# Keys' features in blocks of 432 keys, and two layer norms applied on GpSimd from SBUF

## The chip, the cores and the metric

The kernel runs on one core of a Trainium2 chip. The time is the device time of one execution in microseconds. A "slot", a "unit" and a "batch" below are stretches of this kernel's own main loop.

## What is computed

The input is x of shape (8, 128, 36, 36) in float32: 8 batches, 128 channels, N = 1296 positions. Two layers follow one another; only what the change touches is kept here.

```python
# layer 0: group norm, then convolutions with softmax attention; its sum with x
x = x + conv_attention(group_norm(x))
t = tokens(x)                                # (8, 1296, 128)
# layer 1, first half: additive attention over all pairs of tokens
h = layer_norm(t)                            # mean and variance over the 128 channels
q, k = h @ Wq.T + bq, h @ Wk.T + bk
scores = einsum('bijd,d->bij', tanh(q[:, :, None] + k[:, None]), w) + bw
t = t + softmax(scores) @ h
# layer 1, second half: each of 64 experts takes its best 8 tokens of the batch
h = layer_norm(t)
probs = softmax(h @ gate_w.T, axis=1); topv, topi = top_8(probs)
pooled = sum of topv * h[topi]               # per expert
out = t + scatter(expert_mlp(pooled) * topv)
```

The kernel doesn't evaluate the tanh of every pair. It writes the score as a sum of quotients of products of "features", exponentials of linear maps of the query's and of the key's token. There are NF = 8 groups of 128 features each for queries (`qf`) and for keys (`kf`).

## The kernel before

The main loop goes over 8 batches, 3 chunks of 432 queries (`CH`), and 11 tiles of keys (`KT`): ten of 128 keys and one of 16 (`REM`), which stands sixth in the order. One pass over (batch, chunk, tile) is a unit. A unit of a full tile has 12 slots, that of the small one has two. A batch has 366 slots.

In a slot, TensorE makes two denominators `d` (L910, for three slots ahead, `LAG`) and two numerators `n` (L910); ScalarE takes the logarithm of `d` (L933) and, every second slot, the exponential that inverts (L936); VectorE multiplies `n` by it. In slots 0, 1, 3, 4, 6, 7, 9 and 10 VectorE makes two products into `rp` (L964), and GpSimd adds them to `accp` (L971, L973). In slots 2, 5, 8 and 11 (`DVE_PAIRS`) VectorE also adds, into `accd` (L958, L960), and GpSimd gets no addition. `rp` has three buffers. At a unit's end GpSimd folds the sums (L980, L982), and seven slots later ScalarE makes the weights `e` (L993).

All other work is background, written as Python generators in four lanes: `first_of_all`, `urgent` (attention outputs; for batch 0 also its keys), `gates` (the gating of the batch before), and `background` (layer 0, tokens and keys of the next batch). Each generator yields whether its next step has matmuls and how many slots to rest. `take_turns` (called at the head of a slot) runs steps without matmuls, though not in `DVE_PAIRS` slots except for the first lane. `matmul_turn` (at the end of a slot) runs at most one step with matmuls, paced by a balance of `PACE` = 400 columns a slot. Engines follow the order in which instructions are so recorded, and each engine's queue runs in that order. Matmul results of the background (`aux`) and the numerators `n` share four PSUM banks.

The pieces that the change touches:

- `tokens(b)` turns x into tokens in groups of four transposes (`tpl`, L285), copies them to `tok` in SBUF (L605), takes mean and variance, and has GpSimd raise the variance to the power -1/2 (`ln_rs`, L262). Then it transposes x a second time, two tiles a group (`tpn`), and VectorE normalises from PSUM into `xh` (L640). `xh` is turned back (`tpc`) into `xT`.
- `keys(b, tiles)` makes the keys' features tile by tile: two groups of four matmuls of 128 columns (`pk`, L281), one exponential of 128x512 for each (L684), one write to DRAM (`kd`, L695). For the small tile GpSimd writes two masked copies (L689). The loop's `prefetch` reads a tile back as `kf` (L893), 4 KB a row, two units ahead.
- `gate_logits(b, chunks)` turns the tokens after attention (`t2`) to `t2T` (L790), writes that to DRAM, turns it back two tiles a group (`tp`, L285), and VectorE normalises from PSUM (L800), which needs GpSimd's power `t_rs` (L262). Then it is turned again for the gate's logits.
- `query_block` makes the next chunk's query features in the last units of a chunk: ScalarE L707, GpSimd L708. L372 scales a weight on GpSimd. L468 is layer 0's exponential, `px` one of its matmuls of 432 columns.
- `inner(g)` adds the experts' first bias by a matmul with 16 rows of `ident`.

Before the loop the kernel makes batch 0's tokens, the keys of the first three tiles and three query blocks; the other eight tiles' keys go into `urgent`.

Of the kernel before, what the change touches and what calls it, by code (L numbers as in the profile page):

```python
# [16 lines left out]
N = H * W  # L17
# [53 lines left out]
def kernel(  # L71
# [41 lines left out]
        return t  # L113


    kd = [dram.tile([NKT, 128, NF * 128], F32, tag=f"kd{b % 2}", name=f"kd{b}") for b in range(NB)]
# [10 lines left out]
    with ExitStack() as loop, ExitStack() as score:  # L127
# [139 lines left out]


        TAKE = (False, 1)

        def step(rest=1):
            return (False, rest)
# [311 lines left out]
        prepared, made = {}, set()  # L584

        def tokens(b):

# [39 lines left out]
            rsqrt(rs, ve)  # L627
            xh = big_tile("xh")[:, : NKT * (C + 1)].rearrange("p (t c) -> p t c", c=C + 1)
            nc.gpsimd.memset(xh[:, :, C : C + 1], 1.0)
            yield matmuls(3)  # L630
            for g in range(0, NKT, 2):
                tp = aux("tpn")
                some = list(range(g, min(g + 2, NKT)))
                for t in some:
                    o, n = KT[t]
                    turned_to(tp[:n, (t - g) * C : (t - g + 1) * C], r[:, o : o + n], ident)
                yield TAKE
                for t in some:
# [25 lines left out]
        def keys(b, tiles):  # L664

            xT = prepared[b][1]
            yield matmuls(1)
            for t in tiles:
                o, n = KT[t]
                first = (b, t) == (0, order[0])  # L670
                if first:
                    kf_of[0] = kfp.tile([128, NF, 128], F32, tag="kf", name="kf")
                for q0 in (0, NF // 2):
                    some = slice(q0, q0 + NF // 2)
                    pk = aux("pk1").rearrange("p (q t) -> p q t", t=128)
                    for q in range(NF // 2):
                        bmm(pk[:, q, :n], a_k[:, (q0 + q) * 128 : (q0 + q + 1) * 128],
                           xT[:, o : o + n], start=True, stop=True)
                    yield TAKE
                    if first:  # L680
                        ks = kf_of[0][:, some, :]
                    else:
                        ks = kstp.tile([128, NF // 2, 128], F32, tag="ks", name="ks")
                    nc.scalar.activation(ks[:, :, :n], pk[:, :, :n], AF.Exp)  # L684
                    kd3 = kd[b][t].rearrange("p (q t) -> p q t", t=128)[:, some, :]
                    if n == REM:

                        for x in range(2):
                            nc.gpsimd.tensor_scalar(  # L689
                                ks[:, :, (x + 1) * n : (x + 2) * n], ks[:, :, :n],  # L690
                                pairs[:, min(q0, 1), x : x + 1], None, ALU.mult,
                            )
                        nc.sync.dma_start(kd3[:, :, : 2 * n], ks[:, :, n : 3 * n])
                    else:
                        nc.sync.dma_start(kd3, ks)  # L695
                    if q0 > 0:
                        made.add((b, t))
                    yield matmuls()

        def query_block(b, c, q, qf):  # L700

# [61 lines left out]
        def gate_logits(b, chunks):  # L763


            t2, mv = attended[b]
            if b not in logits:
                logits[b] = (
                    big_tile("probs")[:E, :N],
                    small.tile([E, NCH], F32, tag="mx", name="mx"),  # L770
                )
            pr, mx = logits[b]
            tiles = range(chunks[0] * TPC, (chunks[-1] + 1) * TPC)
            yield step()
# [12 lines left out]
            for c in chunks:  # L787
                tp, tt = turned(c, "t2T")
                yield TAKE
                nc.vector.tensor_copy(tt, tp[:, :CH])  # L790
                nc.sync.dma_start(t2d[b][:, c * CH : (c + 1) * CH], tt)
                yield matmuls(1)
                for j0 in range(0, TPC, 2):
                    tp = aux("tp3")
                    for j in (j0, j0 + 1):
                        turned_to(tp[:T, j * C : (j + 1) * C], tt[:, j * T : (j + 1) * T], ident)
                    yield TAKE
                    for j in (j0, j0 + 1):
                        t = c * TPC + j
                        nc.vector.tensor_scalar(  # L800
                            t2[:T, t, :], tp[:T, j * C : (j + 1) * C],
                            mv[:, t, 0:1], rs[:, t - tiles[0] : t - tiles[0] + 1],
                            ALU.subtract, ALU.mult,
                        )
                    yield matmuls()
            for c in chunks:
                tp, xc = turned(c, "xc")
                yield TAKE
                nc.vector.tensor_copy(xc, tp[:, :CH])
                yield matmuls(2)  # L810
                pg = aux("pg")
                bmm(pg[:E, :CH], gw_s, xc, start=True, stop=True)
                yield TAKE
                nc.vector.tensor_scalar(
                    pr[:, c * CH : (c + 1) * CH], pg[:E, :CH], gb_s, None, ALU.add, ALU.max,
                    accum_out=mx[:, c : c + 1],
                )
                yield matmuls()
# [68 lines left out]
        def prefetch(u):  # L887
            if u < len(units) and u not in kf_of:
                b, c, j = units[u]
                assert (b, j) in made  # L890
                n = 128 if j < NKT - 1 else 32
                kf = kfp.tile([128, NF, 128], F32, tag="kf", name="kf")
                nc.sync.dma_start(  # L893
                    kf[:, :, :n], kd[b][j].rearrange("p (q t) -> p q t", t=128)[:, :, :n]
                )
                kf_of[u] = kf

# [231 lines left out]

        urgent.run(len(slots))  # L1130
        experts = [load_experts(g) for g in range(4)]
        b1_s = biases.tile([NGR, EG, HID], F32, tag="b1", name="b1_s")
        nc.sync.dma_start(b1_s, weight1[:, 128, :].rearrange("(g q) h -> g q h", q=EG))
# [28 lines left out]
    def inner(g):  # L1162
        ph = aux("phid")
        for q in range(EG):
            mm(ph[32 * q : 32 * q + 32, :], pooled_s[:, g * EG + q, :], experts[g][0][:, q, :],
               start=True, stop=False)
        of_group = ident[:NGR, g : g + 1].to_broadcast([NGR, 32])
        for q in range(EG):
            mm(ph[32 * q : 32 * q + 32, :], of_group, b1_s[:, q, :], start=False, stop=True)
# [122 lines left out]
```

## Time and profile before

| | |
|---|---|
| median of 3 runs | 6157.78 us (6153.82 to 6159.6) |
| the profiled execution's own time | 6152.63 us |
| its span, first to last instruction | 6150.6 us |
| granted TensorE clock, mean | 0.986 |
| first numerator of the loop starts at | 158.8 us |
| batch 6, from its first numerator to batch 7's | 736.4 us |
| batch 7, the same to its last numerators | 653.9 us |

In the profile PE is TensorE's matmuls, PEld its weight loads, DVE VectorE, ACT ScalarE, POOL GpSimd and SP the engine that issues the DMAs. A row of a timeline has start, length, engine, line, operation and tiles; the bracket is the idle time before it and who ended that. A row of groups has count, busy time, mean time of one in ns, and idle time before. Rows of stretches have the length, then busy time and count by engine, then granted clock, share of DMA and GB/s.

### The profile page before, as it was taken

How to read it: one execution, taken by the hardware profiler on the slowest of the kernel's cores; microseconds unless marked ns; L12 is line 12 of the kernel's file. 1: busy time of each engine (PE TensorE's matmuls, PEld its weight loads, DVE VectorE, ACT ScalarE, POOL GpSimd, SP SyncE). 2: the span in 40 equal slices, each digit the busy share in tenths (PEclk: the TensorE clock that was granted, in tenths of full speed). 3: DMA queues.
4: the chain of work that ended last, by engine and by line, in shares of the span. 5: the costliest groups of instructions: out<-in, count | busy, mean ns of one | idle time of the engine just before them, and what ended most of it. 6: DMA issues, size and time to landing. Idle time of an engine off the chain costs nothing.

```text
span 6150.6 us, 93223 instructions
## 1 busy us (share of the span) xinstructions
PE 5963.4 (97%) x33576; PEld 2866.4 (47%) x33576; DVE 4798.4 (78%) x9518; ACT 5281.1 (86%) x5371; POOL 4597.5 (75%) x2804
## 2 busy tenths in 40 slices
PE   7999999999999999999999999999999999999996
PEld 5454444544544445444445444454454444544443
DVE  4787878878787787877888777887778878788872
ACT  1888898888988899888998899888898888999980
POOL 4777777777778777878687777877777777787870
PEclk9999999999999999999999999999999999999997
DMA  1200011000210001100111001100021000100017
GB/s 47 71 33 22 25 62 52 20 25 28 72 38 24 26 32 64 42 22 23 49 52 37 22 20 63 45 33 22 28 71 39 24 26 27 61 29 29 25 71 262
DMA packets 150239, 270.88 MB, mean 44 GB/s; under 512 B 45392, under 2 KB 74960, under 8 KB 149776
## 3 DMA queue, kind: packets, MB, share of 16 engines
q1 hardware_dynamic: 149776, 264.92, 12.9%
q8 instruction: 265, 4.34, 0.3%
q14 instruction: 198, 1.62, 0.1%
HBM read 200.41 MB, written 64.19 MB: 43 GB/s over the span
## 4 chain that ended last, share of the span: by engine, by line
PE 76%; ACT 8%; DVE 6%; issue 6%; POOL 2%; DMA 1%; SPq 1%; POOLq 0%; DVEq 0%; ACTq 0%
PE n L910 37%; PE d L910 12%; PE pa L281 7%; ACT lq L933 6%; PE pc L281 5%; PE s L281 3%; PE pk L281 3%; PE pq L281 3%; DVE rp L964 2%; DVE n L958 1%; DVE accd L960 1%; PE d L915 1%; ACT lq L936 1%; PE n L915 1%; ACT e L993 1%
## 5 line engine op out<-in xcount | busy, mean ns | idle before, releaser
L973 POOL TENSOR_TENSOR accp<-accp,rp 128x864 f32<-128x864 f32 x1440 | 2917.0, 2026 | 1032.0 <-DVE rp L964 938.9
L910 PE MATMUL n<-qf,kf 32*128 32x432 f32 (+1 forms) x11520 | 3320.8, 573 | 47.6 <-ACT e L993 13.3
L910 PE MATMUL d<-qf,kf 32*128 32x432 f32 (+1 forms) x11520 | 2983.8, 560 | 39.5 <-ACT lq L933 38.9
L933 ACT ACTIVATE lq<-d 128x864 f32<-128x864 f32 x2928 | 2525.3, 879 | 531.2 <-PE d L910 502.6
L964 DVE TENSOR_TENSOR rp<-n,lq 128x432 f32<-128x432 f32 x3912 | 2174.4, 600 | 739.8 <-PE d L910 539.9
L936 ACT ACTIVATE lq<-lq 128x1728 f32<-128x1728 f32 (+1 forms) x1464 | 2398.2, 1638 | 46.3
L910 PEld LDWEIGHTS n<-qf,kf 32*128 32x128 f32 (+1 forms) x11520 | 1207.1, 184 | 1603.2 <-DVE rp L964 584.0
L910 PEld LDWEIGHTS d<-qf,kf 32*128 32x128 f32 (+1 forms) x11520 | 1088.6, 185 | 420.9 <-issue 225.0
L958 DVE TENSOR_TENSOR n<-n,lq 128x432 f32<-128x432 f32 x1440 | 815.2, 608 | 138.7 <-PE n L910 83.7
L960 DVE TENSOR_TENSOR accd<-n,accd 128x432 f32<-128x432 f32 x1440 | 867.4, 602 | 24.7
L971 POOL TENSOR_TENSOR accp<-rp 128x864 f32<-128x864 f32 x240 | 485.5, 2023 | 194.7 <-DVE rp L964 192.0
L708 POOL TENSOR_SCALAR qf<-qf,cs_s 128x432 f32<-128x432 f32 x192 | 261.2, 1366 | 45.1 <-ACT qf L707 44.4
L281 PEld LDWEIGHTS pa<-xh,e 128*108 128x108 f32 x1920 | 226.1, 176 | 123.7 <-DVE rp L964 53.3
L982 POOL TENSOR_TENSOR accd<-accp,accd 128x432 f32<-128x432 f32 x240 | 265.3, 1106 | 18.8
L980 POOL TENSOR_TENSOR accp<-accp 128x432 f32<-128x432 f32 x240 | 264.6, 1103 | 16.7
L281 PE MATMUL pa<-xh,e 128*108 128x129 f32 x1920 | 265.4, 286 | 6.0 <-DVE accd L960 3.1
L281 PE MATMUL s<-q,k 128*116 128x432 f32 x480 | 230.3, 568 | 1.7 <-DVE q L313 1.4
L281 PEld LDWEIGHTS pk<-xT,a_k 128*128 128x128 f32 x1408 | 171.4, 192 | 107.0 <-DVE n L958 33.7
L459 POOL TENSOR_TENSOR tot<-tot,e 116x432 f32<-116x432 f32 x192 | 212.2, 1105 | 6.0 <-ACT e L468 4.6
L468 ACT ACTIVATE e<-s 116x432 f32<-116x432 f32 x240 | 125.0, 521 | 96.7 <-PE s L281 96.3
L281 PE MATMUL pa<-e,vw 116*128 116x432 f32 x480 | 204.6, 549 | 0.0
L281 PE MATMUL pk<-xT,a_k 128*128 128x128 f32 (+1 forms) x1408 | 202.6, 287 | 0.1
(212 smaller groups left out, 3786.5 us busy)
## 6 DMA issues: line engine op xcount, KB each, us to landing
kf<-kd SPq DMA_DIRECT2D x239, 512.0 KB
kd<-ks SPq DMA_DIRECT2D x158, 256.0 KB
w<-in_weight_dram SPq DMA_DIRECT2D x32, 1024.0 KB
wk_t<-wk_t_d SPq DMA_DIRECT2D x7, 768.0 KB
wv_t<-wv_t_d SPq DMA_DIRECT2D x7, 768.0 KB
wq_t<-wq_t_d SPq DMA_DIRECT2D x7, 768.0 KB
x<-in_x_dram SPq DMA_DIRECT2D x8, 648.0 KB
t<-tokd SPq DMA_DIRECT2D x96, 54.0 KB
```

The costliest lines, as they stand in the source:

```text
L281: mm(out, lhsT, rhs, **kw)
L708: nc.gpsimd.tensor_scalar(qf[:, 1, :], qf[:, 0, :], cs_s[:, q : q + 1], None, ALU.mult)
L910: mm(outs[h][:, :CH], kf[rows[h], q, :], qf_of[b, c, q][rows[h], part, :], start=True, stop=True)
L933: nc.scalar.activation(lq[:, o : o + n, :], d[:, :n, :CH], AF.Ln)
L936: nc.scalar.activation(some, some, AF.Exp, scale=-1.0)
L958: mult(ns[h], ns[h], lq[:, o + h, :])
L960: nc.vector.tensor_add(live["d"], ns[h], live["d"])
L964: mult(rp[:, h, :], n, lq[:, o + h, :])
L971: nc.gpsimd.tensor_add(live["p"], live["r"], rp)
L973: nc.gpsimd.tensor_add(live["p"], live["p"], rp)
L980: nc.gpsimd.tensor_add(s[:, 0, :], s[:, 0, :], s[:, 1, :])
L982: nc.gpsimd.tensor_add(d, s[:, 0, :], d)
```

## The change

`keys` now takes a range of keys instead of tiles: for each of the 8 groups of features one matmul of up to 432 columns, one exponential and one write. `kd` is laid out by features and keys, so that a tile is read back in rows of 512 B. The small tile's two masked copies go to a tile of their own (`kr`), written once to `krd`, in 16 GpSimd operations of 16 columns instead of 4 of 64. Batch 0's first four tiles are made before the loop, by one call for 128 keys and one for 384; the rest are three generators in `urgent`.

`tokens` normalises `tok` from SBUF by GpSimd, and `gate_logits` normalises `t2` in place by GpSimd (the very last chunk by VectorE). The second transposes are gone. These steps yield a new mark, `ASIDE`, and run after the `take_turns` of `DVE_PAIRS` slots alone. The experts' first bias is kept as 64 rows and added by a matmul with 64 rows.

```diff
+        ASIDE = (None, 1)
...
             xh = big_tile("xh")[:, : NKT * (C + 1)].rearrange("p (t c) -> p t c", c=C + 1)
             nc.gpsimd.memset(xh[:, :, C : C + 1], 1.0)
-            yield matmuls(3)
-            for g in range(0, NKT, 2):
-                tp = aux("tpn")
-                some = list(range(g, min(g + 2, NKT)))
-                for t in some:
-                    o, n = KT[t]
-                    turned_to(tp[:n, (t - g) * C : (t - g + 1) * C], r[:, o : o + n], ident)
-                yield TAKE
-                for t in some:
-                    n = KT[t][1]
-                    nc.vector.tensor_scalar(
-                        xh[:n, t, :C], tp[:n, (t - g) * C : (t - g + 1) * C],
-                        mv[:n, t, 0:1], rs[:n, t : t + 1], ALU.subtract, ALU.mult,
-                    )
-                yield matmuls()
+            yield ASIDE
+            for t, (o, n) in enumerate(KT):
+                nc.gpsimd.tensor_scalar(
+                    xh[:n, t, :C], tok[:n, t, :], mv[:n, t, 0:1], rs[:n, t : t + 1],
+                    ALU.subtract, ALU.mult,
+                )
+                if t % 3 == 2 or t == NKT - 1:
+                    yield ASIDE if t < NKT - 1 else step()
...
+        def keys(b, lo, hi):
...
+            for q in range(NF):
+                pk = aux("pk1")[:, :n]
+                bmm(pk, a_k[:, q * 128 : (q + 1) * 128], xT[:, lo:hi], start=True, stop=True)
+                yield TAKE
+                ks = kf_of[0][:, q, :] if first else kstp.tile(
+                    [128, CH], F32, tag="ks", name="ks")[:, :n]
+                nc.scalar.activation(ks, pk, AF.Exp)
+                nc.sync.dma_start(kd[b][:, q, lo:hi], ks)
+                if hi == N:
+                    for x in range(2):
+                        nc.gpsimd.tensor_scalar(
+                            kr[:, q, x, :], ks[:, n - REM :],
+                            pairs[:, q // (NF // 2), x : x + 1], None, ALU.mult,
+                        )
+                yield matmuls()
+            if hi == N:
+                nc.sync.dma_start(krd[b], kr.rearrange("p q x t -> p q (x t)"))
...
                 nc.sync.dma_start(t2d[b][:, c * CH : (c + 1) * CH], tt)
-                yield matmuls(1)
-                for j0 in range(0, TPC, 2):
-                    tp = aux("tp3")
-                    for j in (j0, j0 + 1):
-                        turned_to(tp[:T, j * C : (j + 1) * C], tt[:, j * T : (j + 1) * T], ident)
-                    yield TAKE
-                    for j in (j0, j0 + 1):
-                        t = c * TPC + j
-                        nc.vector.tensor_scalar(
-                            t2[:T, t, :], tp[:T, j * C : (j + 1) * C],
-                            mv[:, t, 0:1], rs[:, t - tiles[0] : t - tiles[0] + 1],
-                            ALU.subtract, ALU.mult,
-                        )
-                    yield matmuls()
+                yield matmuls()
+            yield ASIDE
+            eng = nc.vector if chunks[0] == NCH - 1 else nc.gpsimd
+            for c in chunks:
+                for t in range(c * TPC, (c + 1) * TPC):
+                    eng.tensor_scalar(
+                        t2[:T, t, :], t2[:T, t, :], mv[:, t, 0:1],
+                        rs[:, t - tiles[0] : t - tiles[0] + 1], ALU.subtract, ALU.mult,
+                    )
+                yield ASIDE if c < chunks[-1] else step()
+            yield matmuls(1)
...
             for lane in lanes:
-                if lane.due(p, False) and (k not in DVE_PAIRS or lane is first_of_all):
+                if k not in DVE_PAIRS or lane is first_of_all:
+                    if lane.due(p, False):
+                        lane.run(p)
+                elif lane.due(p, None):
                     lane.run(p)
...
-        drain(tokens(0), keys(0, order[:1]))
+        drain(tokens(0), keys(0, 0, 128))
...
-        drain(keys(0, order[1:3]))
+        drain(keys(0, 128, 512))
         prefetch(1)
-        urgent.append(keys(0, order[3:]))
+        for lo, hi in ((512, 896), (N - REM, N), (896, N - REM)):
+            urgent.append(keys(0, lo, hi))
...
-                            (normal(b + 1), conv_keys(b + 1), layer0(b + 1), tokens(b + 1),
-                             keys(b + 1, range(NKT)))
+                            (normal(b + 1), conv_keys(b + 1), layer0(b + 1), tokens(b + 1))
+                            + tuple(keys(b + 1, o, o + CH) for o in range(0, N, CH))
```

More of the change, by code (lines that the diff above doesn't have):

```diff
@@ L113, in loaded @@
         return t
-    kd = [dram.tile([NKT, 128, NF * 128], F32, tag=f"kd{b % 2}", name=f"kd{b}") for b in range(NB)]
+    kd = [dram.tile([128, NF, N], F32, tag=f"kd{b % 2}", name=f"kd{b}") for b in range(NB)]
+    krd = [dram.tile([128, NF, 2 * REM], F32, tag=f"krd{b % 2}", name=f"krd{b}") for b in range(NB)]
     tokd = [dram.tile([N, C], F32, tag=f"tokd{b % 2}", name=f"tokd{b}") for b in range(NB)]
@@ L582, in features @@
             feat.update(cs_s=cs_s, fb_s=fb_s, eb_s=eb_s)
-        prepared, made = {}, set()
+        prepared, made, covered = {}, set(), {}
         def tokens(b):
@@ L662, in tokens @@
             prepared[b] = (xh, xT, xr)
-        def keys(b, tiles):
+        def keys(b, lo, hi):
             xT = prepared[b][1]
-            yield matmuls(1)
[L668 to L678, printed above, removed]
-                    yield TAKE
[L680 to L691, printed above, removed]
-                            )
[L693 to L697, printed above, removed]
-                    yield matmuls()
@@ new lines, in keys @@
+            n = hi - lo
+            first = b == 0 and lo == 0
+            if first:
+                kf_of[0] = kfp.tile([128, NF, 128], F32, tag="kf", name="kf")
+            if hi == N:
+                kr = one.tile([128, NF, 2, REM], F32, tag="kr", name="kr")
+            yield matmuls(1)
+            for q in range(NF):
[13 more added lines that the diff above has]
+                yield matmuls()
@@ L700, in query_block @@
+            if hi == N:
+                nc.sync.dma_start(krd[b], kr.rearrange("p q x t -> p q (x t)"))
+            done = covered.setdefault(b, set())
+            done.update(range(lo, hi))
+            made.update((b, t) for t, (o, m) in enumerate(KT) if done.issuperset(range(o, o + m)))
         def query_block(b, c, q, qf):
@@ L791, in gate_logits @@
                 nc.sync.dma_start(t2d[b][:, c * CH : (c + 1) * CH], tt)
-                yield matmuls(1)
-                for j0 in range(0, TPC, 2):
-                    tp = aux("tp3")
-                    for j in (j0, j0 + 1):
-                        turned_to(tp[:T, j * C : (j + 1) * C], tt[:, j * T : (j + 1) * T], ident)
-                    yield TAKE
-                    for j in (j0, j0 + 1):
-                        t = c * TPC + j
-                        nc.vector.tensor_scalar(
-                            t2[:T, t, :], tp[:T, j * C : (j + 1) * C],
-                            mv[:, t, 0:1], rs[:, t - tiles[0] : t - tiles[0] + 1],
-                            ALU.subtract, ALU.mult,
-                        )
-                    yield matmuls()
+                yield matmuls()
[9 more added lines that the diff above has]
+            yield matmuls(1)
             for c in chunks:
@@ L892, in prefetch @@
                 kf = kfp.tile([128, NF, 128], F32, tag="kf", name="kf")
+                o = KT[j][0]
                 nc.sync.dma_start(
-                    kf[:, :, :n], kd[b][j].rearrange("p (q t) -> p q t", t=128)[:, :, :n]
+                    kf[:, :, :n], kd[b][:, :, o : o + n] if j < NKT - 1 else krd[b]
                 )
@@ L1131 @@
         experts = [load_experts(g) for g in range(4)]
-        b1_s = biases.tile([NGR, EG, HID], F32, tag="b1", name="b1_s")
-        nc.sync.dma_start(b1_s, weight1[:, 128, :].rearrange("(g q) h -> g q h", q=EG))
+        b1_s = biases.tile([E, HID], F32, tag="b1", name="b1_s")
+        nc.sync.dma_start(b1_s, weight1[:, 128, :])
         b2_s = biases.tile([128, O], F32, tag="b2", name="b2_s")
@@ L1166, in inner @@
                start=True, stop=False)
-        of_group = ident[:NGR, g : g + 1].to_broadcast([NGR, 32])
         for q in range(EG):
-            mm(ph[32 * q : 32 * q + 32, :], of_group, b1_s[:, q, :], start=False, stop=True)
+            own = ident[:E, g * EG + q : g * EG + q + 1].to_broadcast([E, 32])
+            mm(ph[32 * q : 32 * q + 32, :], own, b1_s, start=False, stop=True)
         x = hidp.tile([128, HID], F32, tag="hid", name="hid")
```

## The prediction, made before the changed kernel ran

> **What bounds the kernel now.** I read the page's first part, then the busy time by stretch, then timelines, then the groups of instructions. The page's first part seems to name TensorE:
>
> ```profile
> PE 5963.4 (97%) x33576; PEld 2866.4 (47%) x33576; DVE 4798.4 (78%) x9518; ACT 5281.1 (86%) x5371; POOL 4597.5 (75%) x2804
> ```
>
> A stretch of one unit (12 slots; start and end are the first `n` matmul of the unit and of the next, four records of `n` to a slot) says more. The columns are window, length, then busy time of PE, PEld, DVE, ACT and POOL:
>
> ```profile
> 2419.11:2443.65 24.54, 22.95 (x118) 11.15 (x117) 22.55 (x47) 20.64 (x20) 19.69 (x12) 0.93 0.13 40
> 2443.65:2464.88 21.23, 20.86 (x115) 10.18 (x114) 20.64 (x44) 19.61 (x20) 16.92 (x12) 1.00 0.07 17
> 3032.46:3057.74 25.28, 25.28 (x162) 14.39 (x161) 17.48 (x32) 24.71 (x29) 17.45 (x10) 1.00 0.30 107
> 3082.85:3109.70 26.85, 26.82 (x143) 12.58 (x142) 17.38 (x32) 25.94 (x31) 24.81 (x17) 1.00 0.15 51
> 5608.02:5627.98 19.96, 19.25 (x99) 7.68 (x97) 16.73 (x32) 19.77 (x20) 16.77 (x10) 1.00 0.05 9
> ```
>
> The last is a bare unit of batch 7 with no background work: ScalarE is busy 99%, so 20 us a unit is ScalarE's floor, though PE looks 96% busy. The first two are the gating's (batch 3, chunk 0, tiles 2 and 3): ScalarE idles 3.9 and 1.6 us there. The third and fourth hold the keys: ScalarE is at 98% and 97%, and in the fourth GpSimd at 92%. The cause of the gating's idle time, from the timeline:
>
> ```profile
> 2424.02 2.30 POOL L262 TENSOR_TENSOR t_rs<-ve,neg_half 108x12 f32<-108x12 f32 x1
> ...
> 2426.36 0.73 DVE L800 TENSOR_SCALAR t<-tp,t_mv,t_rs 108x128 f32<-108x128 f32 x2 [0.90 <-POOL t_rs L262]
> ...
> 2427.14 1.65 PE L910 MATMUL n<-qf,kf 32*128 32x432 f32 x3 [1.20 <-DVE t L800]
> ...
> 2429.25 0.89 ACT L933 ACTIVATE lq<-d 128x864 f32<-128x864 f32 x1 [1.85 <-PE d L910]
> ```
>
> VectorE's normalisation (L800) waits for GpSimd's power; it holds a bank that the next `n` needs, TensorE waits 1.20 us, ScalarE 1.85 us.
>
> **What the Trainium skill says.** (1) "Trainium Kernel Development and Optimization", Performance Expectations: matmul busy time is a bad metric, because matmuls are pipelined. The trace agrees: 96% busy in the bare unit. (2) "TensorE: Matmul & The Clock Gate", Part 4: a transpose's output goes to PSUM, so a VectorE pass must follow. The trace agrees: each removed pair of transposes has its L640 or L800. (3) "GPSIMD Engine Reference", 4.1 Engine selection, calls GpSimd roughly line-rate for one-input elementwise work. The trace doesn't agree for this form: L708 takes 1366 ns for 432 elements and L372 612 ns for 128, some 2.5 ns an element. I take the trace.
>
> **The change part by part.** Prices of TensorE groups are from the first matmul to the next `n` or `d`, in the timeline:
>
> ```profile
> 703.01 0.99 PE L281 MATMUL px<-xpad,w_h 128*128 128x432 f32 x2
> 703.93 0.63 PE L910 MATMUL n<-qf,kf 32*128 32x432 f32 x2
> ...
> 758.57 0.44 PE L285 MATMUL tpn<-ident,x 128*128 128x128 f32 x2
> 758.94 1.08 PE L910 MATMUL n<-qf,kf 32*128 32x432 f32 x2
> ...
> 3050.53 1.16 PE L281 MATMUL pk<-xT,a_k 128*128 128x128 f32 x8
> 3051.61 0.63 PE L910 MATMUL n<-qf,kf 32*128 32x432 f32 x2
> ```
>
> So a pair of transposes is 0.37 us, a group of four 128-column matmuls 1.08, one 432-column matmul 0.92. How much of TensorE's time is paid? Batch 6 takes 736.4 us with 212 us of such background groups (summed from the timeline), batch 7 takes 653.9 with 71: 82.5 / 141 = 0.58 us paid per us. I use 0.58 where nothing nearer is seen.
>
> *Gating* (7 batches). Six pairs of transposes go: 6 x 0.36 = 2.2 us of TensorE, and 12 x 0.40 (L800) = 4.8 us of VectorE. The wait shown goes too: GpSimd now normalises behind its own power, holding no bank. 2.2 x 0.58 + 1.2 (TensorE's wait) = **-2.4 us**. Added: 12 GpSimd operations on 108x128 with subtract and multiply. The trace has no such form. Below: 0.61 us (L372, one operation); above: 1.22, twice that. I take 0.7, since the fixed part isn't paid twice. In the changed program's order they stand at the heads of slots 32, 35 and 38 of the batch, in which VectorE adds for itself. GpSimd had 19.69 + 16.92 = 36.6 us of work in these two units; 12 x 0.7 makes it 45.0. The units would take 45.8 - 2.4 = 43.4, and two `rp` buffers of 2.03 us let GpSimd lag by 4.1. It just fits: nothing paid, but what is late next is `accp`, queued behind four normalisations; `rp` on VectorE waits for it.
>
> *Tokens* (7 batches in the background). Six groups go: 6 x 0.37 = 2.2 us of TensorE, 11 x 0.40 (L640) of VectorE: 2.2 x 0.58 = **-1.2**. The 11 GpSimd operations (7.7 us, slots 300 to 311) fall in three units (tiles 4, 10 and 5 of the last chunk) where GpSimd was busy 16.3 + 4.1 + 15.0 = 35.4 of 49.4 us, and with 7.7 more would be at 43.1: hidden. Without that cover they would cost up to 7.7.
>
> *Keys* (7 batches). TensorE: 22 groups, 20 of 1.08 and two smaller, 23.8 us in all, become 24 x 0.92 = 22.1. ScalarE: 20 x 0.59 + 2 x 0.21 become 24 x 0.52 (L468, 432 columns): +0.4. ScalarE is at 98%, so I count -1.6 x 0.58 + 0.4, rounded up for the saturation: **-0.2**. GpSimd: 4 x 0.45 (L689) become 16 on 16 columns, 0.33 each (the line through 64 and 128 columns): +3.5 us, three pairs of them in the unit that has it at 92%, the other five in slack. Queued behind them are `accp` and the queries' L708. I count 1 us more there, less 0.4 for the two groups of keys that no longer run over into the next batch: **+0.6**. Bounds: 0 to +3.5.
>
> *DMA.* 64 KB more are written per batch, in 25 issues of some 0.3 us on SP instead of 22; a tile of keys is read in rows of 512 B instead of 4 KB. SP's next reads stand behind each write that still waits for its exponential, as before. The queue's packets took 12.9% of the engines' span, and a tile is asked for two units (40 us) ahead: nothing. If that cover were gone, a late tile would stop both kinds of products, unit by unit.
>
> *Start.* Nothing covers it. L640 took 3.59 us for 11; GpSimd takes 7.7: +4.1. The first tile's keys have the same columns as before (3.36 us of TensorE), with eight short exponentials instead of two behind them: +0.2. Then three tiles instead of two ahead of the loop: 3.84 us of TensorE become 8 x 0.84 (384 columns): +2.9; the loop has two groups fewer, 2 x 1.08 x 0.58 = -1.2. Sum **+6.0**. Batch 0: the changed order puts ten groups of keys into slot 30 at once, 8 x 0.84 + 2 x 0.27 = 7.3 us of TensorE, in which ScalarE has ten exponentials (4.2) and then idles: +3.1, less 1.0 for lighter slots before: **+2**.
>
> *End.* VectorE's four operations still wait for the power at 5995.94, but no transposes stand between: **-0.5**. The expert bias has 64 rows instead of 16 under the same 512 columns, beside waits for weights: 0 (uncovered also near 0, as columns set a matmul's time).
>
> Sum: 7 x (-2.4 - 1.2 - 0.2 + 0.6) = -22.4; +6.0 + 2 - 0.5 = **-15 us**. The profiled execution took 6152.63 us (span 6150.6, 2.0 outside), 5.2 under the median 6157.78; so 6137.6 for it and 6143 for the median.
>
> **Rivals.** *All of it is paid.* If the slots run at TensorE's and VectorE's pace, a batch gives 2.2 + 2.2 + 1.6 of TensorE and the 1.2 wait, 7.2 us: -50 + 7.5 = 6115. For it: the gating's VectorE at 92%. Against: ScalarE at 97% with the keys.
>
> *GpSimd's wait takes the place of VectorE's.* Its 45 us leave the gating's two units no room and the keys' copies delay the batch's end; of 3.2 us a batch 2.2 are given back: -7 + 7.5, 6158, no change. For it: GpSimd runs from 3083 to 3118 nearly without a gap. Against: its idle time elsewhere.
>
> *Slower: two operations cost as two instructions, 1.22 us each.* The gating's units then ask 36.6 + 14.6 = 51.2 us of GpSimd against 43.4 + 4.1: 3.7 us lost a batch; the start pays 13.4 - 3.6 = 9.8 instead of 4.1. 7 x (-3.2 + 3.7) + 11.7 + 2 - 0.5 = +17: 6175. It decides from about 1.03 us an operation (no gain); from 1.15 it is slower by over 0.2%.
>
> **How the numbers follow.** Forecast 6143 (own range 6128 to 6155): 0.50. All paid 6115: 0.20. Given back 6158: 0.17. Slower 6175: 0.13. A measurement here can tell about 0.2% (12 us) from no change: below 6145.5 is faster, above 6170 slower. Faster: 0.20 + about two thirds of 0.50 = 0.53. Slower: 0.13 and some of the third case, 0.16. Same: 0.31. Leaving out some 0.1 at each end gives 6106 to 6176.
>
> **What would show it.** Right: normalisations of 0.6 to 0.8 us on GpSimd; units 2 and 3 of a batch's first chunk near 43.4 us together with ScalarE's 1.85 us gap gone; the keys' units at 24 to 27 us with ScalarE at 97%; the first `n` near 166 us instead of 158.8. Wrong: VectorE's `rp` waiting for `accp` by more than 1 us a batch, normalisations over 1 us, or a keys' unit that gets shorter by more than 1 us.

## The result and the profile after

| | before | after |
|---|---|---|
| median of four runs each, same chip | 6155.80 us (6150.04 to 6159.60) | 6223.92 us (6220.60 to 6226.07) |
| profiled execution | 6152.63 us, span 6150.6 | 6226.07 us, span 6224.4 |
| first `n` | 158.8 us | 169.6 us |
| loop, from the first `n` to the end of the last slot | 5814.9 us | 5885.3 us |
| of it, TensorE granted half its clock | 62.6 us | 161.4 us |

The ratio is 1.0113, with a 95% interval of 1.0100 to 1.0126. The change costs 68 us, where the forecast was a gain of 15 us in a range that ended at 6176. The last two rows are added up from the starts of the `n` matmuls and from the clock records of the two traces. "Half clock" is time in which TensorE was granted 0.50 of its clock.

The totals of the page hide it. Its first part after the change:

```profile
PE 5969.4 (96%) x32400; PEld 2758.5 (44%) x32400; DVE 4751.2 (76%) x9338; ACT 5284.7 (85%) x5403; POOL 4757.9 (76%) x3080
```

TensorE has 1,176 instructions fewer, VectorE 180 fewer and 47 us less work, as meant. GpSimd has 160 us more, and yet stands at 76% of the span. The loss is seen by unit. These are the two units of the gating in batch 3 again (chunk 0, tiles 2 and 3), then tile 2 of the last batch's chunk 1, all after the change, and below them that last tile before it. The columns are window, length, busy time of PE, PEld, DVE, ACT and POOL, then the granted clock:

```profile
2456.58:2477.91 21.33, 20.27 (x113) 9.88 (x113) 21.04 (x43) 20.12 (x20) 20.37 (x15) 1.00 0.18 57
2477.91:2504.71 26.80, 23.89 (x111) 10.21 (x110) 19.24 (x39) 20.64 (x21) 26.15 (x21) 0.87 0.04 7
5656.10:5683.30 27.20, 22.54 (x107) 8.83 (x106) 18.62 (x36) 19.27 (x20) 20.86 (x15) 0.81 0.10 28
```

```profile
5587.84:5608.02 20.18, 19.77 (x111) 8.78 (x110) 19.62 (x40) 19.26 (x20) 17.38 (x11) 1.00 0.11 39
```

Tile 2 became shorter, 21.3 us instead of 24.5: VectorE's wait for the power is gone, as forecast. Tile 3 became longer, 26.8 instead of 21.2, and GpSimd is busy in 26.15 of its 26.80 us. In this one unit GpSimd, at 76% of the span, is the bound. The last batch's tile took 20.2 us before at full clock, and takes 27.2 at 0.81 now. The durations of one normalisation on GpSimd (minimum, median, maximum, in ns), and the timeline of tile 3, GpSimd first:

```profile
L789 POOL TENSOR_SCALAR t<-t,t_mv,t_rs x92: 785/797/816, 985.4 to 5895.9; 108x128 f32<-108x128 f32 x92
```

```profile
2481.80 3.14 POOL L789 TENSOR_SCALAR t<-t,t_mv,t_rs 108x128 f32<-108x128 f32 x4
2484.89 1.11 POOL L970 TENSOR_TENSOR accp<-accp 128x432 f32<-128x432 f32 x1
2486.08 1.10 POOL L972 TENSOR_TENSOR accd<-accp,accd 128x432 f32<-128x432 f32 x1
2487.14 2.01 POOL L961 TENSOR_TENSOR accp<-rp 128x864 f32<-128x864 f32 x1
...
2489.18 1.12 DVE L954 TENSOR_TENSOR rp<-n,lq 128x432 f32<-128x432 f32 x2 [4.18 <-POOL accp L961]
2489.85 0.59 PE L287 MATMUL tp<-ident,t 108*128 108x108 f32 x4 [2.61 <-DVE rp L954]
...
2493.80 0.89 ACT L923 ACTIVATE lq<-d 128x864 f32<-128x864 f32 x1 [4.37 <-PE d L900]
```

Four normalisations take 3.14 us. The sum of the next tile's products (L961) stands behind them and behind the last tile's two closing sums (L970, L972). VectorE cannot write its next `rp` before that sum has read the old one and waits 4.18 us, TensorE waits 2.61 us for the bank that `rp` frees, ScalarE 4.37 us for `d`. The waits over the whole span, total, times and longest:

```profile
ACT lq L923 <- PE d L900: 543.0, 633, 5.5
...
DVE rp L954 <- POOL accp L961: 47.8, 19, 4.6
```

The second wait was 6.9 us in five cases before, the first 502.6 us with a longest of 3.3. In the last batch it is TensorE that waits directly (timeline of tile 2 of chunk 1):

```profile
5668.22 3.13 POOL L789 TENSOR_SCALAR t<-t,t_mv,t_rs 108x128 f32<-108x128 f32 x4
...
5669.07 0.44 PE L287 MATMUL tp<-ident,t 108*128 108x108 f32 x1 [2.71 <-POOL t L789]
...
5672.55 1.70 PE L283 MATMUL pg<-xc,gate_w 128*64 128x432 f32 x2 [0.70 <-DVE xc L798]
...
5676.12 0.89 ACT L923 ACTIVATE lq<-d 128x864 f32<-128x864 f32 x1 [5.51 <-PE d L900]
```

`pg`, two matmuls, takes 1.70 us here and 0.94 in the same place before. The same stretch cut into windows shows why, in the clock column (before the last two numbers):

```profile
5663.00:5666.40 3.40, 3.36 (x19) 1.20 (x16) 2.83 (x6) 3.37 (x4) 3.24 (x3) 1.00 0.01 2
5666.40:5669.40 3.00, 0.33 (x1) 0.18 (x1) 1.97 (x4) 2.97 (x4) 3.00 (x3) 0.82 0.00 0
5669.40:5672.40 3.00, 1.44 (x4) 0.55 (x3) 0.51 (x1) 1.22 (x2) 3.00 (x4) 0.50 0.00 0
5672.40:5675.90 3.50, 3.35 (x10) 0.80 (x10) 0.76 (x3) 0.00 (x0) 0.92 (x1) 0.50 0.02 5
5675.90:5678.90 3.00, 3.00 (x16) 1.23 (x12) 2.19 (x5) 0.89 (x1) 1.54 (x1) 0.56 0.00 0
5678.90:5683.30 4.40, 4.21 (x26) 1.63 (x24) 3.87 (x9) 4.26 (x5) 2.48 (x2) 1.00 0.00 0
```

A stall is paid a second time: TensorE comes back at half clock, for 10.2 us here. The Trainium skill has this in "TensorE: Matmul & The Clock Gate", Part 1: after an idle window of about 3.4 us the clock is halved, and a busy window brings it back. The traces agree on the two levels and the window: all half-clock stretches of the two loops are at 0.50, and last 3.41 us or a multiple. They don't agree that a whole window must be idle, which the last section counts.

Where the 73.8 us of the two profiled spans are (sums of unit lengths): start +10.8; batch 0 +8.5; batches 1 to 6: first chunks +38.0, second +23.1, third -13.8; batch 7 +14.4; end -7.4. I don't count the end as an effect of the change: it varies between 169 and 177 us among all the kernels below, with 70 to 102 us at half clock, and does so between kernels that have the same code there.

### The profile page after: what moved, and what is told of

It is laid out like the page before. It is cut to its first block, busy times and chain, and to the rows that moved or that the text cites. A ratio compares the mean times of both kernels' runs of the same rounds, so it can differ in the third digit from the quotient of the medians.

```text
span 6224.4 us, 91148 instructions
## 1 busy us (share of the span) xinstructions
PE 5969.4 (96%) x32400; PEld 2758.5 (44%) x32400; DVE 4751.2 (76%) x9338; ACT 5284.7 (85%) x5403; POOL 4757.9 (76%) x3080
## 3 DMA queue, kind: packets, MB, share of 16 engines
q8 instruction: 255, 4.18, 0.3%
## 4 chain that ended last, share of the span: by engine, by line
PE 73%; ACT 7%; DVE 6%; issue 6%; POOL 5%; DMA 1%; SPq 1%; POOLq 0%; DVEq 0%; ACTq 0%
PE n L900 35%; PE d L900 12%; PE pa L283 7%; ACT lq L923 5%; PE pc L283 5%; PE s L283 3%; DVE rp L954 3%; PE pk L283 2%; PE pq L283 2%; POOL accp L963 2%; DVE n L948 1%; PE d L905 1%; PE n L905 1%; DVE accd L950 1%; PE px L283 1%
## 5 line engine op out<-in xcount | busy, mean ns | idle before, releaser
L900 PE MATMUL n<-qf,kf 32*128 32x432 f32 (+1 forms) x11520 | 3357.8, 576 | 63.6 <-DVE rp L954 22.9
L900 PEld LDWEIGHTS n<-qf,kf 32*128 32x128 f32 (+1 forms) x11520 | 1223.8, 185 | 1766.6 <-DVE rp L954 694.2
L961 POOL TENSOR_TENSOR accp<-rp 128x864 f32<-128x864 f32 x240 | 485.5, 2023 | 229.1 <-DVE rp L954 228.1
L972 POOL TENSOR_TENSOR accd<-accp,accd 128x432 f32<-128x432 f32 x240 | 265.4, 1106 | 18.8
L970 POOL TENSOR_TENSOR accp<-accp 128x432 f32<-128x432 f32 x240 | 264.9, 1104 | 15.0
L943 DVE TENSOR_TENSOR accd<-n,lq 128x432 f32<-128x432 f32 x240 | 144.7, 603 | 75.3 <-ACT lq L926 47.0
L283 PE MATMUL pk<-xT,a_k 128*128 128x432 f32 (+3 forms) x416 | 192.5, 554 | 2.4 <-ACT ks L676 2.4
```

The lines of the kernel that those rows point to most:

```text
L283: mm(out, lhsT, rhs, **kw)
L900: mm(outs[h][:, :CH], kf[rows[h], q, :], qf_of[b, c, q][rows[h], part, :], start=True, stop=True)
L961: nc.gpsimd.tensor_add(live["p"], live["r"], rp)
L970: nc.gpsimd.tensor_add(s[:, 0, :], s[:, 0, :], s[:, 1, :])
L972: nc.gpsimd.tensor_add(d, s[:, 0, :], d)
```

## The experiments

The twelve ran in three groups of four, in the order of the table, each group beside the kernel before on one chip. There the kernel before had medians of 6152.3, 6153.6 and 6152.9 us, against 6155.8 beside the changed kernel. So a difference between a kernel here and the changed kernel, or between two groups, is uncertain by some 3 us. The ratios are to the kernel before in the same group; "half clock" is that of the loop.

| kernel | median us | ratio to before, interval | first `n` | loop | half clock |
|---|---|---|---|---|---|
| gating alone | 6241.89 | 1.0144 (1.0130 to 1.0158) | 161.8 | 5904.6 | 184.3 |
| tokens alone | 6179.94 | 1.0047 (1.0034 to 1.0061) | 167.4 | 5838.5 | 119.5 |
| keys alone | 6164.55 | 1.0018 (1.0011 to 1.0024) | 163.3 | 5828.8 | 110.0 |
| gating on VectorE | 6255.28 | 1.0172 (1.0158 to 1.0185) | 169.0 | 5926.8 | 196.3 |
| own pace | 6214.37 | 1.0097 (1.0083 to 1.0111) | 167.8 | 5869.9 | 143.4 |
| two by two | 6276.55 | 1.0193 (1.0178 to 1.0209) | 168.4 | 5947.3 | 227.1 |
| tokens and keys | 6176.17 | 1.0035 (1.0023 to 1.0048) | 169.3 | 5832.5 | 102.4 |
| busy wait | 6219.38 | 1.0106 (1.0092 to 1.0120) | 169.8 | 5877.4 | 119.5 |
| batch 0 undone | 6154.79 | 1.0002 (0.9994 to 1.0011) | 163.3 | 5816.2 | 100.1 |
| batch 0 undone, later | 6199.19 | 1.0072 (1.0059 to 1.0085) | 160.9 | 5854.6 | 128.0 |
| before, later | 6217.76 | 1.0106 (1.0093 to 1.0120) | 162.3 | 5876.4 | 137.8 |
| left out | 6180.95 | 1.0044 (1.0030 to 1.0057) | 168.3 | 5833.8 | 96.6 |

**One part at a time.** Each is the kernel before with the diff's lines for that part; keys alone takes the bias in 64 rows with it, since `kr` needs its room.

> The kernel before, with only the gating's part of the change: its twelve normalisations on GpSimd in SBUF, tokens and keys as before. Theory G (the gating's normalisations come to GpSimd in bursts of four, 3.13 us each, between products; what is queued behind them, the sums of products that free rp and the transposes that TensorE takes in order, stops both kinds of products): this one part makes most of the 68 us. From the trace of after: 7.0 us in each of batch 7's chunks 1 and 2, 1.5 in its chunk 0, and 2.4 to 5.4 in the first chunk of six batches, so +30 to +47 us: 6186 to 6203. Rival K (the keys' blocks and their 512 B rows cost the most, the gating's units only show the wait): under +15 us, below 6171.

> The kernel before, with only the tokens' normalisation on GpSimd. My forecast's terms: the start pays 4.3 us (eleven operations of 0.80 instead of 0.33 on the way to the first product), each of seven batches gains 1.2: -4 us, 6152. Rival (the transposes behind it stop TensorE as in the gating): the first product 4 us later and no gain or a loss in the batches, +4 to +15 us: 6160 to 6171. Which, is read from the last chunks' lengths, 247.7 us each before.

> The kernel before, with only the keys by blocks (and the expert bias in 64 rows, which makes the room in SBUF for the copies of the last 16 keys); tokens and gating as before. Theory G: the start pays 3.4 us, batch 0 about 8 us for the ten groups in one slot, the other batches about nothing: +8 to +15 us, 6164 to 6171. Rival K: +40 us or more, 6196 or more, spread over all batches, with waits for the keys' loads or for GpSimd's copies.

Gating alone costs 89.6 us, tokens 27.7, keys 12.3. So the gating carries most, and rival K falls: keys alone is cheap, and its second chunks (batches 1 to 6) are unchanged at 250.8 us. But gating alone is above its range, tokens are above their rival's range, and the three add to 130 us, not to 68. They don't simply add, which the later runs take up.

**Another engine for the same work.** In the changed kernel:

```diff
-            eng = nc.vector if chunks[0] == NCH - 1 else nc.gpsimd
+            eng = nc.vector
```

> The changed kernel, with the gating's twelve normalisations given to VectorE (0.34 us each, from SBUF, in the same slots, as the change has it for the last chunk already); the six pairs of transposes stay away. Theory G: TensorE's and rp's waits go, batch 7 gives back 13 to 15 us and the first chunks of six batches 3 to 6 us each: -33 to -50 us against after, 6174 to 6191. Rival V (the waits were for order, and VectorE, at 92 to 96% of the first chunks, takes GpSimd's place): within 15 us of after, above 6209. Rival K: -15 us, 6209.

It is 31 us slower still, where theory G expected a gain of 33 to 50 and rival V at most 15 either way. The durations of its L789 (minimum, median, maximum, in ns) and one place in its timeline:

```profile
L789 DVE TENSOR_SCALAR t<-t,t_mv,t_rs x96: 332/339/2177, 981.8 to 6117.2; 108x128 f32<-108x128 f32 x96
```

```profile
5704.47 4.11 POOL L963 TENSOR_TENSOR accp<-accp,rp 128x864 f32<-128x864 f32 x2
...
5705.47 3.71 DVE L789 TENSOR_SCALAR t<-t,t_mv,t_rs 108x128 f32<-108x128 f32 x4
```

Four operations of 0.34 us take 3.71 us and end 0.6 us after GpSimd's two sums. From PSUM the same normalisation took 0.40 us beside GpSimd's sums. The Trainium skill has it in "SBUF — State Buffer", SBUF: two separate sides: VectorE and GpSimd share a pair of SBUF ports under an exclusive lock. It binds VectorE's operations in a mode with two ports, or with two inputs in SBUF, and the one that comes second is blocked for the other's whole instruction. The trace fits this: 41 of the 96 operations took 0.89 to 2.18 us instead of 0.34, and all 41 lay beside a sum on GpSimd; beside GpSimd's short power (L263) none was held up. So this run did not tell theory G from rival V: reading from SBUF, VectorE waits for GpSimd too. Before the change the 96 normalisations from PSUM took 397 to 411 ns each, so the transposes into PSUM had kept VectorE clear of such waits.

**The last batch.** In `attend` of the changed kernel:

```diff
-            if b == NB - 1:
+            if b == NB - 1 and c < NCH - 1:
+                gates.append(gate_logits(b, [c]))
+            elif b == NB - 1:
                 yield from gate_logits(b, [c])
```

> The changed kernel, but the last batch's gating of chunks 0 and 1 is queued as a step of its own instead of at the end of the attention, so that the next tile's exponential no longer forces all of it out at once behind four normalisations on GpSimd. If the 7 us of the last batch's tile 2 come from this forced end: 27.2 us become 21 to 22 in chunks 1 and 2, -10 to -12 us against after, 6212 to 6214. If TensorE waits for the same normalisations wherever they stand: 0 to -4 us, 6220 to 6224.

9.5 us less, just short of the first case. The same tile:

```profile
5653.91:5674.30 20.39, 19.44 (x108) 8.55 (x107) 18.66 (x35) 19.92 (x20) 19.84 (x15) 1.00 0.14 39
```

20.4 us instead of 27.2, at full clock, with the same four normalisations on GpSimd. It was the forced end: `exps` empties `urgent` before its second exponential of a chunk, and the change had pushed the transposes so far back that they were issued there, straight behind the normalisations. By the traces the last batch became 15.1 us shorter, more than the change had added to it, and the end after the loop, which varies, 5 us longer. So the total lies near the forecast in part by chance.

**Smaller bursts.** In the changed kernel the gating yields after every second normalisation instead of every fourth:

```diff
+                    if t % 2 == 1 and t < (chunks[-1] + 1) * TPC - 1:
+                        yield ASIDE
-                yield ASIDE if c < chunks[-1] else step()
+            yield step()
```

> The changed kernel, but the gating's normalisations go to GpSimd in twos (six slots, a unit and a half) instead of in fours (three slots). Burst theory: 1.6 us at a time leaves rp's buffers their lag; the first chunks of six batches go from 244 to 239 to 241 us, with fewer half-clock stretches of TensorE in tile 3 (two or three of 3.4 us now): -20 to -30 us, 6194 to 6204. Rival (the sum on GpSimd counts, 9.6 us wherever it stands): within 8 us of after, 6216 to 6232.

52.6 us slower than after. My burst theory falls, and the rival's 6216 to 6232 is missed by far too. Tiles 3 and 4 of batch 3's first chunk:

```profile
2488.29:2508.86 20.57, 19.48 (x103) 8.56 (x103) 17.43 (x35) 19.95 (x20) 20.15 (x17) 1.00 0.05 8
2508.86:2542.87 34.01, 28.44 (x138) 11.99 (x137) 21.30 (x42) 20.49 (x21) 29.17 (x28) 0.85 0.06 16
```

Tile 3 is back at 20.6 us, but GpSimd is busy in 20.15 of them and carries its backlog into tile 4, where the next batch's copies into `xwin` (0.55 us each) wait in the same queue; tile 4 takes 34.0 us instead of 23.6. So smaller bursts alone don't help: the same work, spread over six slots, meets what comes behind it in GpSimd's queue. How much of the loss is the queue and how much the half clock (0.85 in tile 4) isn't separated.

**Without the gating's part.** The changed kernel with `gate_logits` as before:

> The changed kernel with the gating as before (six pairs of transposes, normalised by VectorE from PSUM): tokens and keys as changed. Alone the two cost 27.7 and 12.3 us. If costs simply add: 6192. If what each costs alone is largely the same thing, TensorE falling to half clock in tile 2 of a first chunk while the gating waits for the power, it is paid once: some 15 us less, 6177. The forecast's arithmetic without any clock: start +8, batch 0 +2, seven batches of -0.8: 6157.

6176.2 us. So inside the changed kernel the gating's part costs 47.8 us, tokens and keys 22.6, not 40. The forecast of 6177 was met by luck, since its reason doesn't hold: the loss in tile 2 isn't paid once, but hardly at all. Over the first chunks of the six batches, tile 2 costs 9.6 us more than before in tokens alone, 13.4 in keys alone, and 2.2 with both.

**Keeping TensorE busy.** In the changed kernel, ahead of the transposes that wait in the last batch:

```diff
+                if b == NB - 1 and name == "xc" and c < NCH - 1:
+                    for _ in range(7):
+                        mm(tp[:, :CH], ident, a_k[:, :CH], start=True, stop=True)
```

> The changed kernel, with seven needless matmuls (128x432, into the bank that the transposes fill next) ahead of the waiting transposes in the last batch's chunks 0 and 1: TensorE has something to do while GpSimd normalises; the result is not touched. Clock theory (a stall of some 3 us costs 7 because TensorE comes back at half clock for 7 to 10 us): tile 2 of chunks 1 and 2 goes from 27.2 to 23 to 25 us at a clock near 1.0; 6216 to 6220. Rival (the wait itself costs 7 us): 27 us or more, 6224 to 6228.

```profile
5652.85:5677.96 25.11, 23.70 (x121) 10.39 (x120) 18.55 (x36) 19.35 (x20) 20.43 (x15) 1.00 0.11 31
```

The clock stays at 1.00, and the tile takes 25.1 us instead of 27.2, although the needless matmuls run 0.6 us past GpSimd's last normalisation. The clock's share of the 7 us is thus at least 2.1 us, more than a quarter of them; the rest goes with the wait and the forced order. It is just outside the upper end of what the clock theory expected: the direction holds, I had its size too large. The total, 4.5 us less, is near what these runs can tell.

**The start and batch 0.** The kernel with tokens and keys as changed, and in it:

```diff
-                nc.gpsimd.tensor_scalar(
+                (nc.vector if b == 0 else nc.gpsimd).tensor_scalar(
...
-            while urgent and len(es.get((b, c), ())) == 1:
+            while urgent and len(es.get((b, c), ())) == 1 and (b, c) != (0, 0):
```

> Tokens and keys as changed, gating as before, and two things of batch 0 undone: its tokens are normalised by VectorE (from SBUF, GpSimd has nothing else to do then), and its ten groups of keys are no longer forced into one slot, but queued one by one. If the start and batch 0 carry what the two parts lose (10.5 us to the first product, 8.4 in batch 0, of 22.6): the first product near 163, batch 0 near 744 instead of 750 us, 6162 to 6167 in all, against 6176. If the loss sits in the later batches: 6172 to 6176.

21.4 us less, and below the range that I gave. The first `n` is at 163.3 us instead of 169.3, and batch 0 takes 734.5 us instead of 750.5. But that isn't a loss that is simply taken back: the kernel before needs 742.1 us for batch 0, so the unforced order gains 7.6 us there. Batches 1 to 6 stay 9.8 us longer than before. The slot with the ten forced groups, after the change and here:

```profile
228.04:238.54 10.50, 8.14 (x31) 4.13 (x30) 2.39 (x7) 6.98 (x13) 6.20 (x10) 1.00 0.27 88
```

```profile
221.67:223.55 1.88, 1.88 (x11) 0.90 (x10) 1.85 (x5) 1.65 (x4) 1.88 (x3) 1.00 0.02 4
```

The forced slot after the change has a wait that the forecast left out. In it and just behind it ScalarE waits three times, 3.8 us in all, until the DMA has written one of the three buffers of `ks`, and TensorE waits for ScalarE. Two more such waits, 2.2 us, stand around the first `n`; the kernel before has none.

This version is the best of all tried, and no better than the kernel before.

**The old wait.** In two kernels the gating's first transposes come two slots later, so that the power is ready:

```diff
-                yield matmuls(1)
+                yield matmuls(3 if c == chunks[0] and b < NB - 1 else 1)
                 for j0 in range(0, TPC, 2):
```

> As the kernel with batch 0 undone, and the gating's first pair of transposes two slots later, so that GpSimd's power is ready when VectorE comes to it. Clock theory: tile 2 of the first chunks loses its wait of 1.2 to 1.85 us and the 3.4 us of half clock that follow it in every second batch or more: 2 to 4 us in each of six batches, 6142 to 6155. Rival (the wait is only moved): 6160 to 6167.

> The kernel before, with only the gating's first pair of transposes two slots later. Clock theory: tile 2 of a first chunk goes from 23.8 and 24.5 us to 21.5 to 22.5, no half clock there: 6139 to 6148. Rival (the wait is only moved to the next slots): within 4 us of before, 6150 to 6158.

Both are slower, by 44.4 us against the kernel with batch 0 undone and by 64.8 against before. Neither theory had that. In the kernel before with this edit, tile 2 of batch 3 is 24.4 us as it was, and tile 3 24.1 instead of 21.2. Other background moves too: over the six batches 864 instead of 792 of the convolutions' matmul records (`pc`) fall in the first chunks, and the second chunks take 253.0 us instead of 250.8. The wait for the power was cheap, and moving it is dear; what in the new order makes it dear isn't shown.

**What the normalisations cost.** In the changed kernel the loop over tiles is empty for GpSimd:

```diff
-                for t in range(c * TPC, (c + 1) * TPC):
+                for t in range(c * TPC, (c + 1) * TPC if eng is nc.vector else 0):
```

> The changed kernel with the gating's normalisations on GpSimd left out (all but the last chunk's four, so the gating works on tokens that aren't normalised); order, transposes and all else stay. If GpSimd's 9.6 us a batch are what the gating's part costs: first chunks at 236 to 238 us instead of 244, tile 2 of the last batch's chunks 1 and 2 near 21 to 24, 6166 to 6180. If the cost lies in the new order (the background work that moves forward, the forced end): 6200 or more.

43.0 us less than after, 6181, at the edge of the first case. Tile 3 of batch 3, first chunk:

```profile
2465.36:2486.39 21.03, 20.73 (x111) 9.43 (x110) 19.14 (x39) 20.41 (x21) 18.50 (x13) 1.00 0.05 8
```

Tile 3 falls from 26.8 to 21.0 us, and in that chunk no other unit changes by more than 0.03 us. Over the span VectorE's wait of `rp` for `accp` falls from 47.8 to 20.0 us. So the gating's loss goes when GpSimd's 12 operations go, to within some 5 us. In the last batch they need the forced end beside them: there the run with its own pace lost nothing on balance (655.2 us for the batch, 655.9 before) with the operations in place. The run shows a second thing: with normalisation for nothing, the gating's new order still isn't faster than the old one (6181 against 6176 for tokens and keys alone). Its first chunks save 5.3 us in six batches and its third chunks 10.9, but the second chunks take 254.3 us each instead of 250.9. The removed transposes were also what held the background back. Over the six batches, 72 matmul records of the convolutions (`pc`) move from the second chunks to the first, and 96 of layer 0's attention (`s` and `pa`) from the third to the second. Why the second chunks pay more for it than the others gain isn't shown.

## Why the prediction was wrong

**The gating's sum on GpSimd: the step that failed.** The forecast said of tiles 2 and 3 "It just fits: nothing paid", from 45.0 us of GpSimd's work in 43.4 us plus a lag of 4.1. The operation was mis-sized a little (0.80 us instead of 0.7), which gives 46.2 and would still have fitted. What failed is the averaging over two units. The forecast itself put the operations in slots 32, 35 and 38; slot 32 is late in tile 2, and GpSimd came to the first of them at 2474.6 us, 18 us into that tile, although the power was ready at 2463.8. Eight of the twelve fell into tile 3, where GpSimd was then busy 98% of the time. One group of four and two closing sums, 5.3 us, were more than the 4.1 us of lag. The forecast even named the place where it would show, `accp` behind four normalisations, and one of its signs of being wrong came true: `rp` waited for `accp` 47.8 us, far more than 1 us a batch. Leaving the operations out gives 43 us back.

**The gating's gain.** The forecast was -2.4 us a batch. Tile 2 did become 3.2 us shorter in batch 3. But the forecast took 0.58 us for each us of TensorE's work that goes; what the kernel's pacing does with a free turn is to fill it. In the kernel without the normalisations, batches 1 to 6 stand at +0.2 us in the first chunks together, +20 in the second, -8 in the third against before.

**The last batch** had no term at all. Its chunks are gated one by one inside `urgent`, which the next exponential empties by force; two tiles took 7.0 us more each, and taking the gating out of `urgent` made the last batch 15.1 us shorter, the whole kernel 9.5.

**The clock** was in the profile that I quoted and was not read: the row of tile 2 before the change says 0.93. The loop's time at half clock rose from 62.6 to 161.4 us. At most half of these 98.8 us is lost directly, 49 us; the run that kept TensorE busy bounds it from below in one place, 2.1 us for 10.2 us of half clock.

**Start.** The terms that were priced came out in sum: from the last of the tokens' first transposes (`tpl`) on, +4.3 us for the normalisation (forecast 4.1) and +3.4 for the keys (0.2 + 2.9). Of the 3.4, though, 1.1 stand ahead of the first `d`, where 5.1 us instead of 2.8 were at half clock, and 2.3 behind it. Another 3.2 us came before all this, in instructions that the change doesn't touch: six matmuls of `po` took 856 ns instead of 543, at half clock. These 3.2 us aren't the change's. Gating alone and "before, later" have the code of the kernel before up to the first `n`, and their last `tpl` ends at 137.1 and 137.4 us, as late as after the change, against 133.9 in the profile before.

**Batch 0** was priced at +2 and took +8.5. Ten groups forced into one slot were not partly hidden: the slot took 10.5 us where the unforced one takes 1.9. The forecast's "nothing" for the DMA didn't hold for the writes: the 6.0 us that ScalarE waited for them lie here and at the start. For the reads it held: with 512 B rows a load of keys waited 1.4 us in all for its write, against 3.3 before.

**Tokens and keys in the other batches** were priced at -0.8 us each. With batch 0 undone they stand at +1.6 (six batches, +9.8 us against before). "Hidden" didn't quite hold for the GpSimd operations: in these six batches VectorE's `rp` waited 12.5 us for `accp`, against 2.1 before. And half clock rose from 44 to 89 us. How much of the 9.8 us each of the two makes, no run separates.

**The rivals.** "GpSimd's wait takes the place of VectorE's" named what happened in the gating's units, but priced it at a lost gain, not at a loss. "Slower" also had GpSimd's sum in those units, and the wrong point: it was to be slower from 1.03 us an operation, and the kernel is slower at 0.80. "All of it is paid" falls. A slip in the forecast's sums changes nothing: ScalarE's term of the keys comes to +0.3 by its own figures, not +0.4.

What stays open: why gating alone costs 89.6 us but 47.8 inside the changed kernel. Its extra shows in tile 0 of the first chunks (25.8 us in batches 3 to 7, 23.4 after the change) and in the third chunks (247.2 us on average in batches 1 to 6, 245.1 after the change), with 184 us of half clock. That the fixed grid of clock windows meets the stalls differently in each kernel would fit, but no run separates it.

## What to carry to other kernels

An engine at 76% of the span can be the bound of one unit: price added work in the window between what releases it and what waits for it, in queue order, not as an average over its surroundings. Where a planner fills free turns and forces others, a removed instruction frees a turn and doesn't shorten the path; ask what moves into the turn and what will now be forced. And look at the granted clock of each stretch before pricing a stall of TensorE, since its cost doesn't end with the wait.

## What the runs showed of the hardware

Half clock begins and ends on a fixed grid of 3.41 us: in each of the two traces every change lies on one grid, to 0.01 us. I counted the idle time of TensorE in each such window of the loop at full clock, from the traces of before and after. With 1.6 us idle or more, the next window was at half clock in all 24 cases; with 0.8 to 1.6 us in 12 of 53; below 0.8 us in 5 of 3,284. Over all 14 traces it is 159 of 162, 133 of 401 and 67 of 22,924. So idle time of about half a window was nearly always enough.

On GpSimd, subtract and multiply on 128 columns with two scalars from SBUF took 0.80 us, where one operation took 0.61: the second operation cost about a third more, not nothing and not as much again. On 16 columns one operation took 0.33 us (median 331 ns), as estimated.

VectorE reading and writing SBUF for 128 columns took 0.34 us, against 0.40 from PSUM, but 0.89 to 2.18 us in 41 of 96 cases, all beside a GpSimd sum.
